# Attention scores on row tiles of 32: two heads at a time, each in a PSUM bank of its own

## The chip, the core and the metric

One core of one Trainium2 chip runs the whole program in one launch. The metric is the device time of that core in microseconds, as the median of some runs; one execution more is profiled, and all durations come from that one. A time is told from another of this kernel by about one per cent.

## What is computed

Four sequences of 256 tokens with 512 features go through two layers. In layer 0 a latent attention and a gated feed-forward net both read the same normalized input, and both are added to it. In layer 1 a selective scan (a state-space model) and a routed mixture of low-rank experts do the same. The change touches the attention of layer 0 only:

```python
C_q  = x @ Wq_d + bq_d                       # 12 latents per token
C_kv = x @ Wkv_d + bkv_d                     # 4 latents per token
q = (C_q @ W_qk + b_qk).reshape(b, s, 32, 4) # 32 heads of 4
scores = einsum('bqhd,bkd->bhqk', q, C_kv) / sqrt(4)
attn = softmax(scores, axis=-1)
V = (C_kv @ Wv_u + bv_u).reshape(b, s, 32, 16)
out = einsum('bhqk,bkhd->bqhd', attn, V).reshape(b, s, 512) @ Wo + bo
```

A head has only four numbers per token, and keys are shared by all heads.

## The kernel before

**Layout.** The 32 heads are four groups `gq` of two halves `hf` of four heads `h4`. A query tile `qs[b]` holds, on 128 partitions, four heads of 32 rows each, for every `gq` and `hf` and all 256 queries; the 32 rows of a head hold its four numbers in high and low parts, and rows for the maximum. The key tile `kms[b]` has four variants, one for each `h4`: variant `h4` is zero outside the 32 rows `32*h4` to `32*h4 + 32`. So a matmul over all 128 rows gives the scores of one head, because the rows of the other three meet zeros. Both are fp32r.

**Two sets of scores.** The scores are made twice. `scores_max` (L324) makes them with queries on the output's partitions, two matmuls of 128 x 512 into one `sc` tile of two banks, and VectorE reduces that to maxima per head (L331). `put_max` (L336) transposes the maxima and subtracts them from the queries. `attend` (L354) then makes the scores transposed, with keys on the partitions: two matmuls of 128 x 512 into one `scT` tile, and one exponential of ScalarE (L363) over both. `weigh` (L365) multiplies the exponentials by the key latents: four matmuls with 32 columns of weights each, one for every `gq`, into four quarters of the partitions of `av`. Each is fp32 and takes two passes in the trace.

**Buffers.** `sc` and `scT` share a pool of two buffers of two banks (`pssc`), so each group of scores waits until the exponential or the reduction two groups before has read its buffer.

**Order.** The order on each engine is written out by hand, as that in which the program is recorded. The feed-forward net is a generator `ff`, and `go(ff, n)` places n steps of it between the attention's instructions; a step of `gate_up` (L403) is two full matmuls of 128 x 512 (L417, the high and low part of the input), a step of `down` (L432) two as well (L442). The scores of block 0 and 2 stand in loops with one or two steps after each group. `attention` (L467) goes through eight steps `k`: `attend`, one step of `ff`, `attend`, one step, then (for blocks 0 and 2) a group of `scores_max` for the next block, `weigh` of the step before, and another group of `scores_max`, then `step - 2` steps of `ff`. `step` is 4, 2, 4 and 4 for the four blocks. `latents` (L269) makes the query and key tiles, with small matmuls of 40, 12 and 8 rows (L289, L296, L310).

After the attention come the projections, the convolution and the scan of layer 1, which the change does not touch.

Of the kernel before, what the change touches and what calls it, by code (L numbers as in the profile page):

```python
# [12 lines left out]
ALU = mybir.AluOpType  # L13
AX = mybir.AxisListType
# [3 lines left out]
P = 128  # L18
B, S, D = 4, 256, 512
# [22 lines left out]
def block_kernel(  # L42
# [25 lines left out]
    mm = nc.tensor.matmul  # L68
# [70 lines left out]
    zk = ap1.tile([P, NTB, 56], F32, name="zk")  # L139
    nc.gpsimd.memset(zk, 0.0)  # L140
    mpl2 = []
    for i in range(2):
        t = ap1.tile([P, 2, 4, 32], F32, name=f"mpl{i}")
# [123 lines left out]
    qs, kms = {}, {}  # L267
# [55 lines left out]

    def scores_max(b, j):  # L324

        gq, hf, qb = j // 4, j // 2 % 2, j % 2
        sc = pssc.tile([P, 2, 512], F32, tag="sc", name="sc")
        for hp in range(2):
            mm(sc[:, hp, :], lhsT=qs[b][:, gq, hf, qb * P : (qb + 1) * P],  # L329
               rhs=kms[b][:, 2 * hp : 2 * hp + 2, :], start=True, stop=True)  # L330
        nc.vector.tensor_reduce(  # L331
            mpl2[b % 2][:, qb, :, 16 + 2 * gq + hf].rearrange("p (a i) -> p a i", a=2),
            sc.rearrange("p a (i k) -> p a i k", i=2), AX.X, ALU.max,
        )

    def put_max(b):  # L336
# [15 lines left out]
    avs, pes = {}, {}  # L352

    def attend(b, k, t):  # L354

        c, h4 = k // 4, k % 4
        if t == 0:
            pes[b, k] = ap1.tile([P, 4, 512], F32, tag="pe", name="pe", bufs=2)
        sc = pssc.tile([P, 2, 512], F32, tag="sc", name="scT")
        for j in range(2):  # L360
            mm(sc[:, j, :], lhsT=kms[b][:, h4, c * P : (c + 1) * P], rhs=qs[b][:, 2 * t + j],  # L361
               start=True, stop=True)
        nc.scalar.activation(pes[b, k][:, 2 * t : 2 * t + 2, :], sc, AF.Exp)  # L363

    def weigh(b, k):  # L365

        c, h4 = k // 4, k % 4
        if k == 0:
            avs[b] = psav.tile([P, 2, S], F32, tag="av", name="av")
        for gq in range(4):  # L370
            mm(avs[b][32 * gq : 32 * gq + 32].rearrange("p a b -> p (a b)"),  # L371
               lhsT=zk[:, 2 * b + c, 24 - 8 * h4 : 56 - 8 * h4], rhs=pes[b, k][:, gq, :],
               start=(c == 0 and h4 == 0), stop=(c == 1 and h4 == 3))

    def normalize(b, ff):
# [91 lines left out]
    def attention(b, ff, after, first, step, side=()):  # L467

        put_max(b)
        go(ff, first)  # L470
        side = list(side)
        for k in range(8):
            attend(b, k, 0)
            go(ff, 1)
            attend(b, k, 1)
            go(ff, 1)
            if after:
                scores_max(b + 1, 2 * k)
            if k:
                weigh(b, k - 1)  # L480
            if after:
                scores_max(b + 1, 2 * k + 1)
            go(ff, step - 2)
            if side:
                f, *args = side.pop(0)
                f(*args)
        go(ff, 1)
        weigh(b, 7)
        go(ff, 1)
        normalize(b, ff)  # L490
# [34 lines left out]
    for j in range(16):  # L525
        scores_max(0, j)
        if j in (4, 8):
            fold_att(j // 8)
            go(ff, 1)
        else:  # L530
            go(ff, 2 if j % 3 else 1)
        if j % 2 == 1:
            go(second, 1)
# [53 lines left out]
    t = w_of["x", 0, 0] = w1.tile([P, 2, HC, P], F32, tag="w_in", name="w_in", bufs=3)  # L587
# [36 lines left out]
    for i in range(2):  # L624
        t = w1.tile([P, 2, KC - 1 + S], F32, name=f"pad{i}")
# [445 lines left out]
    for n in range(NG):  # L1071
        w = slice(n * NB, (n + 1) * NB)
# [32 lines left out]
    for i in range(2):  # L1105
        pdu = psmm.tile([P, 2, S], F32, tag="mm", name="pdus")
        for k in range(2):
            mm(pdu[:, k, :], lhsT=sel[:, (2 * i + k) * P : (2 * i + k + 1) * P], rhs=du[:, 0, :],
               start=True, stop=True)
# [152 lines left out]
    for u in range(total + 2):  # L1262
# [8 lines left out]
        if last >= 0 and last % NU == NU - 1:  # L1271
            c = last % PER // NU
# [9 lines left out]
        if late and u >= total - PER + 22:  # L1282
            c = late.pop(0)
# [113 lines left out]
```

## Time and profile before

| | |
|---|---|
| median of 3 runs | 893.94 us (888.75 to 894.7) |
| profiled execution, its time | 889.37 us |
| its span, first to last instruction | 887.6 us |
| mean granted TensorE clock | 0.927 |
| TensorE matmuls busy | 756.4 us (85%), 3554 |
| VectorE busy | 685.2 us (77%), 675 |
| ScalarE busy | 525.8 us (59%), 1009 |
| GpSimd busy | 489.9 us (55%), 377 |
| scores for the maxima, L329 | 128 matmuls, mean 424 ns |
| transposed scores, L361 | 128 matmuls, mean 408 ns |
| values, L371 | 256 records, mean 605 ns |
| maxima on VectorE, L331 | 64, mean 1222 ns |
| exponentials on ScalarE, L363 | 64, mean 1023 ns |

A matmul's time in such a table runs from its start to the end of its result, so neighbours overlap; what one costs in a row of matmuls is the distance of their starts. "PEld" is the load of the stationary operand, which may run beside a matmul. Rows are written as rows x columns of the stationary tile, then rows x columns that stream: `128*32 128x512` is a tile of 128 rows and 32 columns with 512 columns streamed.

### The profile page before, as it was taken

The page shows a single profiled execution, that of the slowest core. Times are in us where ns is not written, and L with a number is a line of the kernel's source. Part 1 is how long each engine was busy: PE and PEld are TensorE (multiplying, and loading weights), DVE is VectorE, ACT ScalarE, POOL GpSimd, SP SyncE. Part 2 cuts the span into 40 slices and gives each one's busy share as a digit, 9 for nine tenths or more (in the row PEclk, how much of TensorE's full clock was granted, in tenths as well). Part 3 has the DMA queues.
Part 4 walks back from the last instruction along what each step waited for, and adds up shares of the span by engine and source line. Part 5 has one row for each costly group of instructions (what it writes and reads, how often), then busy time and mean ns, then how long its engine had stood idle before and what let it go on. Part 6 is the DMA issues. An engine that isn't in the chain of part 4 may idle for free.

```text
span 887.6 us, 10460 instructions
## 1 busy us (share of the span) xinstructions
PE 756.4 (85%) x3554; PEld 434.2 (49%) x3554; DVE 685.2 (77%) x675; ACT 525.8 (59%) x1009; POOL 489.9 (55%) x377
## 2 busy tenths in 40 slices
PE   5999989999989999998687898668898777965966
PEld 3675555667556576665453444334454433422422
DVE  4695554377565333878999999999999999999995
ACT  4225445312536437678787687776786794855561
POOL 4222222001223242758967789869689759697664
PEclk9999999899999999978997999888999889989896
DMA  6232242001112231374741645341646232426200
GB/s 213 60 95 72 72 119 71 13 1 36 48 48 72 72 116 26 96 185 153 239 111 51 165 120 159 98 127 54 166 134 163 84 96 75 126 72 178 72 24 24
DMA packets 67343, 86.67 MB, mean 98 GB/s; under 512 B 12077, under 2 KB 52025, under 8 KB 66906
## 3 DMA queue, kind: packets, MB, share of 16 engines
q1 hardware_dynamic: 57930, 67.12, 27.0%
q0 software_dynamic: 9072, 18.35, 7.5%
q8 instruction: 28, 0.46, 0.2%
q10 hardware_dynamic: 288, 0.52, 0.2%
q14 instruction: 25, 0.20, 0.1%
HBM read 66.58 MB, written 10.22 MB: 87 GB/s over the span
## 4 chain that ended last, share of the span: by engine, by line
DVE 39%; PE 36%; ACT 11%; POOL 6%; issue 5%; DMA 2%; SPq 0%; DVEq 0%; ACTq 0%; POOLq 0%
DVE h L909 23%; DVE bx L894 8%; ACT decay L888 5%; PE pu L417 5%; PE pg L417 4%; POOL hc L913 4%; PE sc L329 4%; PE av L371 3%; PE po L442 3%; PE scT L361 3%; PE px L696 2%; PE po L1017 2%; ACT pe L363 1%; PE ysum L925 1%; PE pqg L319 1%
## 5 line engine op out<-in xcount | busy, mean ns | idle before, releaser
L913 POOL TENSOR_TENSOR hc<-h,cr 128x1024 f32<-128x1024 f32 (+1 forms) x131 | 301.9, 2307 | 100.6 <-DVE h L909 89.1
L909 DVE TENSOR_TENSOR_SCAN h<-decay,bx 128x1024 f32<-128x1024 f32 (+1 forms) x129 | 288.0, 2234 | 15.6 <-PE po L442 3.9
L888 ACT ACTIVATE decay<-dts,aneg 128x255 f32<-128x255 f32 x504 | 213.6, 498 | 121.0 <-DVE h L909 110.6
L925 PE MATMUL ysum<-hc,stack 128*32 128x256 f32 x1024 | 93.0, 432 | 83.8 <-POOL hc L913 83.6
L894 DVE TENSOR_TENSOR bx<-brow,dus 128x1024 f32<-128x1024 f32 x128 | 157.6, 1231 | 3.7
L429 POOL TENSOR_TENSOR hlo<-g,hhi 128x512 fp32r<-128x512 f32 x28 | 36.1, 1290 | 148.5 <-ACT hhi L428 148.5
L331 DVE TENSOR_REDUCE mpl<-sc 128x4 f32<-128x1024 f32 x64 | 77.2, 1222 | 24.1 <-PE sc L329 23.8
L925 PEld LDWEIGHTS ysum<-hc,stack 128*32 128x32 f32 x1024 | 21.8, 113 | 146.0 <-POOL hc L913 125.5
L400 POOL DMA_DIRECT2D wgu<-in_wgu x56 | 31.2, 557 | 92.7 <-PE pg L417 82.4
L363 ACT ACTIVATE pe<-scT 128x1024 f32<-128x1024 f32 x64 | 62.7, 1023 | 29.9 <-PE scT L361 29.6
L1017 PE MATMUL po<-ow,xc 128*128 128x512 f32 x128 | 73.2, 682 | 2.2 <-DVE xc L929 2.2
L857 PE MATMUL pz<-xn1T,w_in 128*128 128x256 f32 x256 | 67.0, 409 | 0.0
L696 PE MATMUL px<-xn1T,w_in 128*128 128x256 f32 x256 | 64.7, 401 | 0.7 <-DMA w_in<-in_inx 0.6
L696 PEld LDWEIGHTS px<-xn1T,w_in 128*128 128x128 f32 x256 | 51.0, 202 | 20.4 <-issue 11.1
L425 DVE SCALAR_TENSOR_TENSOR g<-g,pg 128x512 f32<-128x512 f32 x28 | 19.2, 685 | 52.0 <-ACT g L424 52.0
L857 PEld LDWEIGHTS pz<-xn1T,w_in 128*128 128x128 f32 x256 | 48.8, 200 | 18.6 <-issue 11.7
L428 ACT CAST hhi<-g 128x512 fp32r<-128x512 f32 x28 | 17.4, 620 | 61.5 <-DVE g L427 61.2
L417 PE MATMUL pg<-xhi,wgu 128*128 128x512 f32 x112 | 47.1, 421 | 5.4 <-issue 2.9
L417 PE MATMUL pu<-xhi,wgu 128*128 128x512 f32 x112 | 47.8, 427 | 1.5 <-DVE g L427 0.7
L442 PE MATMUL po<-wd,hhi 128*128 128x512 f32 x112 | 49.0, 437 | 0.0
L329 PE MATMUL sc<-km,qg 128*128 128x512 f32 x128 | 43.9, 424 | 3.3 <-ACT pe L363 2.8
L417 PE MATMUL pg<-xlo,wgu 128*128 128x512 f32 x112 | 45.7, 408 | 0.0
(225 smaller groups left out, 1256.8 us busy)
## 6 DMA issues: line engine op xcount, KB each, us to landing
dts<-dtd SPq DMA_DIRECT2D x124, 128.0 KB, 2.9
dus<-dud SPq DMA_DIRECT2D x124, 128.0 KB, 2.9
wgu<-in_wgu POOLq DMA_DIRECT2D x56, 256.0 KB, 2.7
w_in<-in_inz SPq DMA_DIRECT2D x16, 512.0 KB, 4.7
w_in<-in_inx SPq DMA_DIRECT2D x15, 512.0 KB, 4.6
dtd<-dt SPq DMA_DIRECT2D x15, 256.0 KB, 2.2
dud<-du SPq DMA_DIRECT2D x15, 256.0 KB, 2.3
wd<-in_wd POOLq DMA_DIRECT2D x7, 512.0 KB, 3.6
```

The costliest lines, as they stand in the source:

```text
L329: mm(sc[:, hp, :], lhsT=qs[b][:, gq, hf, qb * P : (qb + 1) * P], rhs=kms[b][:, 2 * hp : 2 * hp + 2, :], start=True, stop=True)
L331: nc.vector.tensor_reduce(mpl2[b % 2][:, qb, :, 16 + 2 * gq + hf].rearrange("p (a i) -> p a i", a=2), sc.rearrange("p a (i k) -> p a i k", ...
L417: mm(ps, lhsT=wgus[i][:, hc, :], rhs=xs[j][:, hc, :], start=(hc == 0 and j == 0), stop=(hc == HC - 1 and j == 1))
L442: mm(po, lhsT=hids[th][j][:, m, i * P : (i + 1) * P], rhs=wd[:, m, :], start=False, stop=(m == MC - 1 and j == 1))
L696: mm(px[:, i, :], lhsT=w[:, i, hc, :], rhs=xns[b][:, hc, :], start=(hc == 0), stop=(hc == HC - 1))
L857: mm(pz[:, i, :], lhsT=w[:, i, hc, :], rhs=xns[b][:, hc, :], start=(hc == 0), stop=(hc == HC - 1))
L888: nc.scalar.activation(da[:, k, 1:], live["dts", b, c][:, k, 1:], AF.Exp, scale=aneg[:, c, k, g : g + 1])
L894: nc.vector.tensor_tensor(bx, brow[g // 2][:, g % 2, :].unsqueeze(1).to_broadcast([P, NG, S]), live["dus", b, c], ALU.mult)
L909: nc.vector.tensor_tensor_scan(h[:, n].rearrange("p n t -> p (n t)"), da[:, n].rearrange("p n t -> p (n t)"), bx[:, n].rearrange("p n t -> ...
L913: nc.gpsimd.tensor_tensor(hc[:, n], h[:, n], crows[b][:, g, :].unsqueeze(1).to_broadcast([P, NG // parts, S]), ALU.mult,)
L925: mm(ysum[k * NB : (k + 1) * NB, :], lhsT=stack, rhs=hc[:, k, :], start=False, stop=(g == NU - 1))
L1017: mm(live["po", b, i], lhsT=xcs[b][:, c, i * P : (i + 1) * P], rhs=late_w["ow"][:, c, :], start=False, stop=(c == DC - 1))
```

## The change

Every score matmul now takes only the 32 rows of its head, from both operands, instead of all 128 with zeros in the other three quarters.

- In `scores_max` a group holds two heads `2*hp` and `2*hp + 1` in both halves `hf`, instead of four heads in one half. The two heads lie on different rows of the array and go to different banks of `sc` (index `i`), and each half takes 256 columns of a bank. A group has four matmuls of 32 x 256 instead of two of 128 x 512. The reduction reads the same 1024 numbers, and writes four maxima to other places of the same tile.
- In `attend` the two matmuls of a group would have used the same 32 rows. So head `h` is now `(gq + h4) % 4`: the two matmuls use different rows, and each has its own bank as before. `weigh` takes the slice of the key latents that fits that head, so over the steps each `gq` still meets all four heads.

The number of reductions, exponentials and groups, their order on all engines and all transfers are as before. TensorE has 128 matmuls more in its program.

```diff
@@ -323,14 +323,16 @@
 
     def scores_max(b, j):
 
-        gq, hf, qb = j // 4, j // 2 % 2, j % 2
+        gq, hp, qb = j // 4, j // 2 % 2, j % 2
         sc = pssc.tile([P, 2, 512], F32, tag="sc", name="sc")
-        for hp in range(2):
-            mm(sc[:, hp, :], lhsT=qs[b][:, gq, hf, qb * P : (qb + 1) * P],
-               rhs=kms[b][:, 2 * hp : 2 * hp + 2, :], start=True, stop=True)
+        for hf in range(2):
+            for i in range(2):
+                w = slice(64 * hp + 32 * i, 64 * hp + 32 * i + 32)
+                mm(sc[:, i, hf * S : (hf + 1) * S], lhsT=qs[b][w, gq, hf, qb * P : (qb + 1) * P],
+                   rhs=kms[b][w, 2 * hp + i, :], start=True, stop=True)
         nc.vector.tensor_reduce(
-            mpl2[b % 2][:, qb, :, 16 + 2 * gq + hf].rearrange("p (a i) -> p a i", a=2),
-            sc.rearrange("p a (i k) -> p a i k", i=2), AX.X, ALU.max,
+            mpl2[b % 2][:, qb, 2 * hp : 2 * hp + 2, 16 + 2 * gq : 18 + 2 * gq],
+            sc.rearrange("p i (f k) -> p i f k", f=2), AX.X, ALU.max,
         )
 
     def put_max(b):
@@ -353,12 +355,15 @@
 
     def attend(b, k, t):
 
+
         c, h4 = k // 4, k % 4
         if t == 0:
             pes[b, k] = ap1.tile([P, 4, 512], F32, tag="pe", name="pe", bufs=2)
         sc = pssc.tile([P, 2, 512], F32, tag="sc", name="scT")
         for j in range(2):
-            mm(sc[:, j, :], lhsT=kms[b][:, h4, c * P : (c + 1) * P], rhs=qs[b][:, 2 * t + j],
+            h = (2 * t + j + h4) % 4
+            w = slice(32 * h, 32 * h + 32)
+            mm(sc[:, j, :], lhsT=kms[b][w, h, c * P : (c + 1) * P], rhs=qs[b][w, 2 * t + j],
                start=True, stop=True)
         nc.scalar.activation(pes[b, k][:, 2 * t : 2 * t + 2, :], sc, AF.Exp)
 
@@ -368,8 +373,9 @@
         if k == 0:
             avs[b] = psav.tile([P, 2, S], F32, tag="av", name="av")
         for gq in range(4):
+            h = (gq + h4) % 4
             mm(avs[b][32 * gq : 32 * gq + 32].rearrange("p a b -> p (a b)"),
-               lhsT=zk[:, 2 * b + c, 24 - 8 * h4 : 56 - 8 * h4], rhs=pes[b, k][:, gq, :],
+               lhsT=zk[:, 2 * b + c, 24 - 8 * h : 56 - 8 * h], rhs=pes[b, k][:, gq, :],
                start=(c == 0 and h4 == 0), stop=(c == 1 and h4 == 3))
 
     def normalize(b, ff):
```

## Prediction

> **What bounds the kernel now.** The page first: the span, the share of each engine, and the slices.
>
> ```profile
> span 887.6 us, 10460 instructions
> PE   5999989999989999998687898668898777965966
> DVE  4695554377565333878999999999999999999995
> PEclk9999999899999999978997999888999889989896
> ```
>
> One slice is 22.2 us. Slices 2 to 15 (about 28 to 318 us) hold the scores and the attention, and there PE stands at 8 to 9 while DVE is mostly below 8: this part goes at TensorE's pace. From slice 20 on DVE sets the pace, and no edit lies there. So the change is priced on TensorE, stage by stage. The table of stages (us; then busy time of PE, weight load, DVE, ACT, POOL; then granted clock) confirms it:
>
> ```profile
> 28.60:58.90 30.30, 30.10 (x125) 20.47 (x123) 25.08 (x30) 8.48 (x16) 8.11 (x11) 1.00 0.30 87
> 64.10:111.70 47.60, 44.93 (x209) 27.07 (x210) 26.58 (x28) 21.72 (x27) 13.20 (x18) 1.00 0.26 74
> 217.00:262.20 45.20, 44.26 (x203) 25.29 (x202) 25.05 (x26) 21.23 (x26) 11.68 (x15) 1.00 0.22 59
> 271.00:307.00 36.00, 36.00 (x184) 21.76 (x182) 10.92 (x19) 24.30 (x30) 11.73 (x15) 1.00 0.26 69
> ```
>
> These are the scores of block 0, and the attention of blocks 0, 2 and 3. PE is busy 94 to 100%, at full clock. A busy PE includes the tail of each matmul, so prices are read from start to start, in the timeline of TensorE in block 0:
>
> ```profile
> 71.03 0.40 PE L417 MATMUL pu<-xlo,wgu 128*128 128x512 f32 x1
> 71.27 0.62 PE L329 MATMUL sc<-km,qg 128*128 128x512 f32 x2
> 71.83 1.06 PE L371 MATMUL av<-pe,zk 128*32 128x512 f32 x8
> 72.82 0.73 PE L329 MATMUL sc<-km,qg 128*128 128x512 f32 x2
> ...
> 75.94 0.40 PE L417 MATMUL pg<-xlo,wgu 128*128 128x512 f32 x1
> 77.04 0.72 PE L329 MATMUL sc<-km,qg 128*128 128x512 f32 x2 [0.70 <-ACT pe L363]
> ```
>
> Three things are read here. A full 128x512 matmul follows another after 0.23 us, so a group of two scores takes 0.462. The eight av records are four column tiles of 32 in two passes each: 0.99 us from start to start for what would be 8 x 0.43 = 3.4 one after the other, so tiles of different columns do run side by side. And where the shape of the tile changes, time is lost: sc to av takes 0.56 where two matmuls take 0.46, and the first sc behind av lasts longer. The last two lines show a wait: 1.10 us from start to start, of which 0.87 is waiting for the exponential that frees the score buffer.
>
> **The change part by part.** It takes nothing off DVE, ACT, POOL or the queues: 64 maxima over 128x1024 (1.22 us each, L331), 64 exponentials (1.02 us, L363) and the eight av records per step stay, with other columns and another slice of zk. On TensorE 128 full score matmuls L329 become 256 of 32 rows x 256 columns, and 128 of L361 become 128 of 32 rows x 512. The gain would be that two row tiles run side by side; the price is that each group of scores now has another tile shape than the full matmuls around it.
>
> *Price of a change of shape.* Before has matmuls of few rows, too, among full ones (12 rows at L296, 8 at L310):
>
> ```profile
> 19.88 1.12 PE L296 MATMUL pq<-cq,wqk 12*128 12x256 f32 x4
> 20.94 0.50 PE L417 MATMUL pg<-xhi,wgu 128*128 128x512 f32 x1
> 21.28 0.39 PE L417 MATMUL pg<-xlo,wgu 128*128 128x512 f32 x1
> 21.60 0.29 PE L310 MATMUL pz<-cst,kT 8*128 8x8 f32 x2
> 21.98 0.50 PE L417 MATMUL pu<-xhi,wgu 128*128 128x512 f32 x1
> 22.31 0.40 PE L417 MATMUL pu<-xlo,wgu 128*128 128x512 f32 x1
> ```
>
> From 21.28 to 21.60 is 0.32 instead of 0.23: 0.09 in which the array empties. The first full matmul after the change lasts 0.50 instead of 0.40, and the next follows after 0.33 to 0.34 instead of 0.23: 0.105 of weight load that nothing covers. So a change of shape costs 0.196 us, into the small tile and out of it.
>
> *How many.* In TensorE's order of the two programs, by the rows and columns of each stationary tile, the changes of shape up to the last av are 98 before and 304 after: 206 more. By stage: scores of block 0 +26, attention 0 +48, attention 1 and scores of block 2 +52, attention 2 +48, attention 3 +32. Beside av nothing is added (it was another shape already). 206 x 0.196 = 40.4 us more.
>
> *What the pairs save.* No row of before shows two row tiles side by side, so it is bounded: nothing if they run one after the other; half of the group, 0.231 us, if they overlap as the column tiles do. 128 groups x 0.231 = 29.6 us at most. Between the ends lies a load of weights that can't overlap: loads of 128 columns follow each other by 0.11 us (20.94 to 21.05 at L417), so a pair would be 0.107 longer and four small scores 4 x 0.107 = 0.43 instead of 0.231, 64 x 0.107 + 64 x 0.197 = 19.5 us lost again. I take full overlap, since av, the nearest row, has it. The Trainium skill, "TensorE: Matmul & The Clock Gate", section "Measured speedup vs the span model", gives 3.07 times for four row tiles, which no run here shows yet; by it the saving is nearer the full 29.6 than nothing.
>
> *Sum on TensorE:* 40.4 - 29.6 = +10.8 us (by stage +1.4, +2.0, +2.8, +2.0, +2.6).
>
> *What lies beside other work.* Some score groups wait anyway. From start to start such waits make 6.9 us in all: three of 0.87 in attention 0 like the one shown, 0.92 early in attention 2, 0.67 twice in attention 1, and smaller ones. The chain that ends them (tanh, product, copy, exponential on ACT and DVE) starts from a full matmul ahead of the scores and does not move; TensorE arrives later at the wait by two boundaries in and out and two shorter groups, about 0.35 us, and that is hidden. Ten or so waits by 0.3 us make 3 us. If that cover is gone the sum is +10.8; if all waits were cover, +4. I take +8.
>
> *The granted clock.* This is what could make it large. The clock is 1.00 or 0.50 in stretches of 3.41 us, and I set beside each such stretch what TensorE streamed in the one before:
>
> ```profile
> 166.72:170.13 3.41, 3.04 (x13) 1.82 (x13) 1.51 (x4) 0.85 (x2) 0.00 (x0) 1.00 0.00 0
> 170.13:173.55 3.42, 3.40 (x12) 2.54 (x12) 1.72 (x4) 0.62 (x1) 0.00 (x0) 0.50 0.00 0
> ...
> 432.95:436.36 3.41, 1.48 (x7) 0.95 (x5) 3.34 (x4) 3.34 (x9) 3.25 (x4) 1.00 0.99 299
> 436.36:439.77 3.41, 2.18 (x24) 1.31 (x24) 3.31 (x3) 1.52 (x5) 3.41 (x3) 1.00 0.94 398
> ```
>
> The first stretch has PE busy 3.04 us and yet the clock halves after it; the third has 1.48 and keeps it. In the first run four full matmuls (4 x 0.213 = 0.85 us of columns), four of 40 rows (0.43) and four of 12 rows (0.85). Weighted by rows of 128 that is 0.85 + 0.13 + 0.08 = 1.06, a share of 0.31; the third has 6.6 full ones of 0.213, a share of 0.41. Worked out so over all stretches of the trace, the clock fell after each share up to 0.36 and held from 0.38 on; from half clock it rose after 0.74 and more, and stayed after 0.73 and less. A pair of 32-row tiles counts half, so the score groups thin this share. In the steady attention loop after (8 full matmuls 1.71, av 0.85, four pairs 0.43, in 5.6 us) the mean is 0.53, and the leanest 3.41 us, around a wait cut to 0.5 us, have 1.5 / 3.41 = 0.44. The first step of attention 0 and 2 has no av: pair, two full, pair, two full, wait, scores, wait, scores: 1.18 / 3.41 = 0.35. The clock falls if a stretch lies just there (it may begin within some 0.7 of 3.41 us, about 1 in 4 for each block). At half clock the leanest no longer matters but the richest: four full ones and a part of av give 2.4 / 3.41 = 0.71, under 0.74, so it would stay until the attention ends. A step then takes about 9.8 us instead of 5.6: 7 steps x 4.2 = +30 us for that block. The Trainium skill, "TensorE: Matmul & The Clock Gate", section "HAM oscillation — how this bites in real kernels", asks only that TensorE has no idle gap over 3.4 us. There is none here, so by the page the clock costs nothing and the sum stays +8; the stretch at 166.72 speaks against it.
>
> **The rivals.**
> 1. *The clock falls in an attention and stays low:* +8 + 30, 927 on the profiled time, and 957 if in both. For it: the 0.35 above. Against: a small margin over 0.36 suffices, and where stretches begin is chance.
> 2. *Row tiles do not overlap:* the change then does not do what it says. 40.4 - 4 hidden = +36, 925, and pairs at a quarter share would lower the clock as well, 955. For it: no row shows it. Against: av.
> 3. *Faster:* a tile of 64 of 128 rows leaves half the array free, and if weights are loaded there while others stream, a boundary costs only the emptying. 206 x 0.09 = 18.5 - 29.6 = -11 us, 878. It decides from a boundary under 29.6 / 206 = 0.144 us. Against: the first matmul at 20.94 and 21.98 lasts 0.50 although 8 and 12 rows were in use.
>
> **How the numbers follow.** Forecast: overlap, boundaries paid, clock mostly held: 889.37 (profiled time, span 887.6) + 8 = 897.4. The median of the runs, 893.94, lies 4.6 above the profiled one, so as a median I expect 893.9 + 8 = 902. Its own range is 896 to 921 (serial loads at the top). Chances: forecast 0.44, clock 0.38, no overlap 0.10, faster 0.08. The range 891 to 940 leaves out the faster case and the dearest ends of the first two rivals. This kernel can be told from no change by about 1%, 8.9 us: the forecast lies at that line, so half of it counts as the same (0.22), with 0.02 from the faster case; faster 0.06; slower 0.70.
>
> **What would show it.** Right: pairs of L361's successor starting within 0.05 us of each other; the first L417 behind each at 0.50; the attention of block 3 longer by 2 to 3 us; DVE and ACT rows unchanged; the part behind 318 us only shifted. Wrong: pairs 0.2 us apart (rival 2), first full matmuls at 0.40 (rival 3), stages at granted clock well under 0.9 (rival 1).

## The result, and the profile after

The changed kernel is slower: a median of 896.37 us over 20 runs (892.9 to 907.37), beside 890.74 us for the kernel before in the same runs (886.81 to 895.09). The ratio is 1.0064, with a 95% interval of 1.0042 to 1.0086, so about 5.7 us (3.7 to 7.7): clear of no change over these runs, but less than the one per cent by which one time is told from another. Two of the 20 runs, at 905.0 and 907.4 us, had a mean granted clock of 0.919 and 0.914, the others 0.922 to 0.934. The profiled execution took 892.9 us.

The page of the changed kernel: span, TensorE's busy tenths, and the granted clock.

```profile
span 891.1 us, 10715 instructions
PE   5999989999989999998787898677998777965966
PEclk9999999999999999988997999888999889989896
```

The shape is that of before. What is new shows in the table of stages (attention 0 and attention 3):

```profile
64.10:111.70 47.60, 46.48 (x244) 22.20 (x242) 27.53 (x30) 22.22 (x27) 12.97 (x18) 1.00 0.25 73
271.00:307.00 36.00, 36.00 (x171) 16.46 (x174) 10.80 (x19) 23.86 (x28) 10.77 (x14) 1.00 0.24 64
```

In the same 36 us of attention 3 TensorE gets through 171 matmuls where it did 184, at full clock. In attention 0 it is busy 46.48 us instead of 44.93 and does not fall behind: some of its waits are gone. The timeline of TensorE in block 0 says why:

```profile
71.39 0.40 PE L423 MATMUL pu<-xlo,wgu 128*128 128x512 f32 x1
71.72 0.50 PE L366 MATMUL scT<-qg,km 32*128 32x512 f32 x2
72.14 0.50 PE L423 MATMUL pu<-xhi,wgu 128*128 128x512 f32 x1
72.48 0.40 PE L423 MATMUL pu<-xlo,wgu 128*128 128x512 f32 x1
72.81 0.50 PE L331 MATMUL sc<-km,qg 32*128 32x256 f32 x4
73.24 1.07 PE L377 MATMUL av<-pe,zk 128*32 128x512 f32 x8
...
77.67 0.39 PE L423 MATMUL pg<-xlo,wgu 128*128 128x512 f32 x1
78.23 0.50 PE L331 MATMUL sc<-km,qg 32*128 32x256 f32 x4 [0.17 <-ACT pe L368]
```

Both matmuls of a transposed group are one piece of 0.50 us, and in each of the 64 groups they start 3 to 4 ns apart: they run side by side. The group starts 0.33 us after the full matmul ahead of it instead of 0.23, the full one behind it lasts 0.50 and is followed after 0.34 instead of 0.23. From 71.39 to 72.48 is 1.09 us, where four starts 0.231 apart made 0.92. The last two lines are the wait shown for before: 0.56 from start to start, where it was 1.10.

Step by step of the attention (from one start of av to the next), before and after: in attention 0, 4.95 and 5.87 in turn became 5.17 and 5.42; in attention 2, 4.95 and 5.33 became 5.17 and 5.17; attention 1 went from 3.05 to 3.18, attention 3 from 4.00 to 4.30. By stages the span grew by 1.1 us in the scores of block 0, -0.5 in attention 0, +0.4 in attention 1, -0.5 in the scores of block 2, +0.1 in attention 2 and +2.5 in attention 3; the end is 3.5 us later. In the scores of block 2 the kernel before had a stretch of 6.8 us at half clock (from 170 us) and the changed one had none; this helps the changed kernel in the two profiles, and they do lie closer (3.5 us) than the medians.

### The profile page after: what moved, and what is told of

It reads as the page before. It is cut to its first block, busy times and chain, and to the rows that moved or that the text cites. A ratio compares the mean times of both kernels' runs of the same rounds, so it can differ in the third digit from the quotient of the medians.

```text
span 891.1 us, 10715 instructions
## 1 busy us (share of the span) xinstructions
PE 762.0 (86%) x3682; PEld 410.7 (46%) x3682; DVE 685.2 (77%) x675; ACT 527.4 (59%) x1009; POOL 489.9 (55%) x377
## 4 chain that ended last, share of the span: by engine, by line
DVE 39%; PE 34%; ACT 12%; POOL 6%; issue 6%; DMA 2%; SPq 0%; DVEq 0%; ACTq 0%; POOLq 0%
DVE h L915 24%; DVE bx L900 8%; ACT decay L894 6%; PE pu L423 5%; PE pg L423 5%; POOL hc L919 3%; PE av L377 3%; PE po L448 3%; PE sc L331 3%; PE scT L366 2%; PE px L702 2%; ACT pe L368 1%; PE po L1023 1%; DVE px L726 1%; PE pl L274 1%
## 5 line engine op out<-in xcount | busy, mean ns | idle before, releaser
L368 ACT ACTIVATE pe<-scT 128x1024 f32<-128x1024 f32 x64 | 64.3, 1024 | 30.0 <-PE scT L366 29.7
L423 PE MATMUL pg<-xhi,wgu 128*128 128x512 f32 x112 | 52.7, 471 | 5.4 <-issue 2.9
L423 PE MATMUL pu<-xhi,wgu 128*128 128x512 f32 x112 | 52.3, 467 | 1.8 <-DMA wgu<-in_wgu 0.9
L423 PE MATMUL pu<-xlo,wgu 128*128 128x512 f32 x112 | 44.4, 396 | 0.0
```

The source lines that it names most:

```text
L423: mm(ps, lhsT=wgus[i][:, hc, :], rhs=xs[j][:, hc, :], start=(hc == 0 and j == 0), stop=(hc == HC - 1 and j == 1))
```

## The experiments

The theory: each change of tile shape costs 0.196 us, pairs on two row tiles save 0.231 us, and waits for the score buffers cover a part in attention 0 and 2. The rivals: overlap is worth nothing; the cost goes by the number of matmuls; the granted clock is what costs. Ratios are to the kernel before, run beside each experiment. They are not quotients of the medians, and the two can differ by some 2 us (e8 below: 0.9978, although 885.51 stands beside 889.68).

**Each half alone.** e1 keeps the new `attend` and `weigh` and the old `scores_max`; e2 the reverse.

```diff
 # e1: scores_max
-        for hf in range(2):
-            for i in range(2):
-                w = slice(64 * hp + 32 * i, 64 * hp + 32 * i + 32)
...
+        for hp in range(2):
+            mm(sc[:, hp, :], lhsT=qs[b][:, gq, hf, qb * P : (qb + 1) * P],
+               rhs=kms[b][:, 2 * hp : 2 * hp + 2, :], start=True, stop=True)
 # e2: attend and weigh
-            h = (2 * t + j + h4) % 4
-            w = slice(32 * h, 32 * h + 32)
-            mm(sc[:, j, :], lhsT=kms[b][w, h, c * P : (c + 1) * P], rhs=qs[b][w, 2 * t + j],
+            mm(sc[:, j, :], lhsT=kms[b][:, h4, c * P : (c + 1) * P], rhs=qs[b][:, 2 * t + j],
```

> Only the transposed scores are on row tiles; the scores for the maxima are full matmuls as before. Theory (0.196 us for each change of shape, 0.231 us saved by each pair that overlaps, waits of the score buffers cover part of it in attention 0 and 2): 122 changes more x 0.196 - 64 x 0.231 = +9.1 us on TensorE; a step of attention 1 at 3.18 instead of 3.05, of attention 3 at 4.30 instead of 4.00; in attention 0 and 2 about half is covered, so +4 to +6 us against before. Rival (the two edits cost alike, by their number of matmuls): half of the measured +5.6, so +2.8.

> Only the scores for the maxima are on row tiles; the transposed ones are full as before. Theory: 84 changes more x 0.196 - 64 x 0.231 = +1.7 us on TensorE, all of it in the two loops of scores (+1.1 to +1.4 each), and -0.07 us for each step of attention 0 and 2, where they stand beside av, which has another shape anyway. Sum +1 us. Rival (alike by number of matmuls): +2.8 us or more, since this edit has all the 128 matmuls that were added.

e1: 895.27 us, ratio 1.0068 (1.0041 to 1.0094), so +6.0 us. e2: 889.77 us, ratio 1.0012 (0.9989 to 1.0034), so +1.1 us, not told from none. The transposed scores carry the loss, although only the other half has more matmuls than before: it is not their number. Steps in e1: 3.18 in attention 1, 4.30 to 4.33 in attention 3, and 5.23 in attention 0 where before had 4.95; in e2 4.84 there, 0.11 less, because a group beside av pays no additional change on that side. The long steps of attention 0, those with the wait, are 5.87 in e1 as in before, but 5.42 in e2: what made them shorter in the changed kernel is the half with the maxima.

**Overlap taken away.** e3 is the changed kernel with the same head, so the same 32 rows, in both matmuls of a transposed group.

```diff
-            h = (2 * t + j + h4) % 4
+            h = h4
...
-            h = (gq + h4) % 4
+            h = h4
```

> As the changed kernel, but both matmuls of a transposed group take the same head, so the same 32 rows: they can't run side by side. Theory (overlap is what pays for part of the changes of shape): each of 64 groups longer by 0.21 us; steps of attention 1 at 3.6 and of attention 3 at 4.7 us; 13.6 us in all, less what waits cover in attention 0 and 2: +10 to +13 us against the changed kernel, about +17 against before. Rival (a K of 32 alone matters, overlap is worth nothing): no difference to the changed kernel.

It took 931.15 us (907.48 to 937.78, 4 runs), some 35 us over the changed kernel and far more than expected. One of the four took 907.48 us, at a mean granted clock of 0.935: that is 11 us over the changed kernel, as expected. The other three had 0.898 to 0.909, and the profiled execution is one of them. TensorE's timeline in attention 1:

```profile
129.47 0.40 PE L423 MATMUL pg<-xlo,wgu 128*128 128x512 f32 x1
129.79 0.73 PE L366 MATMUL scT<-qg,km 32*128 32x512 f32 x2
130.45 0.50 PE L423 MATMUL pg<-xhi,wgu 128*128 128x512 f32 x1
```

A group now takes 0.66 us to the next start instead of 0.43, and the steps are 3.64 in attention 1 and 4.76 in attention 3, as expected: overlap is worth 0.23 us a group. The rest, in those three runs, is the clock, as the profile of one of them shows. The table of stretches, at the first step of attention 2 and behind it:

```profile
227.87:231.28 3.41, 2.60 (x15) 1.54 (x14) 2.15 (x3) 1.15 (x2) 0.88 (x2) 1.00 0.58 156
...
231.30:289.30 58.00, 58.00 (x167) 25.36 (x166) 19.08 (x19) 15.92 (x18) 7.02 (x9) 0.50 0.11 28
```

The first stretch has a row-weighted share of about 0.35, worked out as in the prediction; then 58 us go at half clock, with a step of attention 2 at 9.9 us, as rival 1 had priced it. The shares in these 58 us are 0.45 to about 0.75, and the clock comes back after one of about 0.77.

**Double the rows.** e4 has the pairs on tiles of 64 rows, half of them zeros, with the heads of a pair in different halves of the array.

```diff
-            h = (2 * t + j + h4) % 4
-            w = slice(32 * h, 32 * h + 32)
+            h = (t + 2 * j + h4) % 4
+            w = slice(64 * (h // 2), 64 * (h // 2) + 64)
...
-                w = slice(64 * hp + 32 * i, 64 * hp + 32 * i + 32)
+                w = slice(64 * i, 64 * i + 64)
```

> As the changed kernel, but with tiles of 64 rows (32 of them zeros), heads paired so that the two are in different halves of the array. Same changes of shape, same overlap, twice the share of rows. Theory: within 1 us of the changed kernel (+5.6 against before), with no run above 900, since the share of rows that holds the clock is far from its limit. Rival (the lower share of rows costs clock in every run): faster than the changed kernel by 3 us or more.

896.05 us, ratio 1.0069 (1.0039 to 1.0098), steps as in the changed kernel to 0.03 us. So the lower share of rows is not what the changed kernel loses by in its median. One of ten runs took 900.9, just over what the theory had named, so that part is not settled.

**What covered the change.** In e5 (from the kernel before) and e6 (from the changed one) half of the exponentials are left out, which shortens each on ScalarE; TensorE's work stays the same.

```diff
-        nc.scalar.activation(pes[b, k][:, 2 * t : 2 * t + 2, :], sc, AF.Exp)
+        nc.scalar.activation(pes[b, k][:, 2 * t : 2 * t + 2, 0:S], sc[:, :, 0:S], AF.Exp)
...
-               ... rhs=pes[b, k][:, gq, :],
+               ... rhs=pes[b, k][:, gq, 0:S].unsqueeze(1).to_broadcast([P, 2, S]),
```

> The kernel before with each exponential over the first 256 of every 512 columns only, and the values made from these columns twice; half of the exponentials are left out. This takes about 0.4 us off each of 64 exponentials, so the waits for the score buffer that end on ScalarE should go: a pair of steps in attention 0 at 9.9 to 10.0 instead of 10.8 us. Theory: 5 us faster than before. Rival (the reductions on VectorE end these waits): no change.

> The changed kernel with the same half of the exponentials left out. Theory (waits for the exponential were the cover that hid the change in attention 0 and 2): without them the difference to the half kernel of before grows to nearly the sum on TensorE, +9 to +11 us, and every step of attention 0 and 2 is 0.2 us longer than there. Rival (the cover lies in the reductions): the difference stays at 4 to 6 us.

e5: 884.51 us, ratio 0.9952 (0.9921 to 0.9984). e6: 893.18 us, ratio 1.0057 (1.0030 to 1.0084). Between them lie 8.7 us by the medians, and 9.3 by the two ratios, instead of 5.7. In attention 2 the steps are 4.92 in e5 and 5.17 in e6: with the waits gone, the change shows in full, 0.25 us a step. In attention 0 e5 has 4.92 and 5.46, not the 9.9 to 10.0 a pair that was expected: half of the wait of 0.87 stays (0.44), and the pair is no shorter than e6's. So the exponentials are the cover in attention 2, and about half of it in attention 0. What the rest is can be read in the traces. These are the links that end the long wait of attention 0, in the kernel before and in the changed one:

```profile
73.59 1.23 DVE L331 TENSOR_REDUCE mpl<-sc 128x4 f32<-128x1024 f32 x1 [0.43 <-PE sc L329]
75.44 0.62 ACT L428 CAST hhi<-g 128x512 fp32r<-128x512 f32 x1 [3.41 <-DVE g L427]
75.97 1.93 ACT L363 ACTIVATE pe<-scT 128x1024 f32<-128x1024 f32 x2
...
74.78 1.22 DVE L333 TENSOR_REDUCE mpl<-sc 128x4 f32<-128x1024 f32 x1 [0.20 <-PE sc L331]
76.63 0.62 ACT L434 CAST hhi<-g 128x512 fp32r<-128x512 f32 x1 [3.35 <-DVE g L433]
77.16 1.93 ACT L368 ACTIVATE pe<-scT 128x1024 f32<-128x1024 f32 x2
```

The chain begins with the reduction of the score group behind av. The product of the feed-forward net stands behind it on VectorE (0.68 us), its copy and then the exponential follow on ScalarE, and only the first exponential frees the buffer. From the start of the reduction to the score matmul that waited it takes 3.45 us in both kernels (73.59 to 77.04, 74.78 to 78.23). In e5 it takes 3.02, shorter by what the exponential lost; the wait that is left lies in the reduction, the product and the copy.

**Another order.** e7 is the control: before, with full matmuls, but in attention 1 and 3 the values of two steps earlier, both transposed groups and the feed-forward steps stand in blocks. e8 has the same order, and row tiles for the transposed scores of these two blocks alone.

```diff
+                if k > 1:
+                    weigh(b, k - 2)
+                attend(b, k, 0)
+                attend(b, k, 1)
+                go(ff, step)
...
 # e8 besides
+            h = (2 * t + j + h4) % 4 if b % 2 else h4
+            w = slice(32 * h, 32 * h + 32) if b % 2 else slice(0, P)
```

> The kernel before (full matmuls), but in attention 1 and 3 the values of two steps earlier come first, then both transposed groups at once, then the feed-forward steps together. The same matmuls and as many changes of shape as before. Theory: the same as before within 1 us; steps at 3.05 and 4.0 us. It is the control for the next one. Rival: with both groups side by side the exponential comes late, and steps of attention 1 get longer by 0.3 us or more.

> The order of the control, and in attention 1 and 3 alone the transposed scores on row tiles as in the changed kernel; all else full as before. Both groups and av now stand together, so a step has one change of shape more than before, for two overlapped pairs. Theory: 0.196 - 0.462 = -0.27 us for each of 16 steps, -4.3 us: steps of 2.8 and 3.75 us, faster than before by 3 to 5 us. Rival (row tiles cost time wherever they are used): slower than the control.

e7: 887.8 us, ratio 0.9981 (0.9960 to 1.0003), steps as before. e8: 885.51 us, ratio 0.9978 (0.9956 to 1.0000): some 2 us faster by the ratio where 3 to 5 were expected, and by the times not told from the control. Its steps are 2.57 and 3.48 us, though, 0.5 shorter than the control's and more than two pairs explain. TensorE in attention 1 of e8:

```profile
128.17 0.53 PE L364 MATMUL scT<-qg,km 32*128 32x512 f32 x4
128.62 0.51 PE L421 MATMUL pu<-xhi,wgu 128*128 128x512 f32 x1
...
129.76 1.07 PE L375 MATMUL av<-pe,zk 128*32 128x512 f32 x8
130.76 0.51 PE L364 MATMUL scT<-qg,km 32*128 32x512 f32 x4
```

All four transposed matmuls are one piece of 0.5 us: their heads lie on four different row tiles, so four run side by side in the time of one. That is 0.69 - 0.196 = 0.49 us a step. In the profiled runs the projections behind the attention begin 5.4 us earlier than before, and the end comes 4.0 us earlier.

**The clock by itself.** e9 is the kernel before with 80 matmuls of 32 x 512 ahead of attention 0, in pairs on two row tiles, and 40 ahead of attention 2 on one.

```diff
+    def rowtest(n, b):
+        ps = [psmm.tile([P, 512], F32, tag="mm", name="rt") for _ in range(2)]
+        for r in range(80 // (3 - n)):
+            i = r % n
+            w = slice(32 * i, 32 * i + 32)
+            mm(ps[i], lhsT=kms[b][w, i, 0:P], rhs=qs[b][w, 0], start=True, stop=True)
```

> The kernel before with 80 more matmuls of 32 rows x 512 columns ahead of attention 0, in pairs on two row tiles, and 40 more ahead of attention 2, all on one row tile; their results are not used. TensorE has nothing else in these stretches of 9 us and is busy all the time. Theory (the clock goes by streamed time weighted by rows, falling under 0.37): pairs have a share of 0.5 and keep 1.00, matmuls start in twos every 0.22 us; singles have 0.25, and after 3.4 to 6.8 us the clock halves and they start every 0.43 us. Rival (the clock goes by busy time, or by idle gaps): 1.00 in both.

One stretch of the pairs, then the first full stretch of the singles and the one behind it:

```profile
65.48:68.89 3.41, 3.41 (x31) 3.04 (x27) 0.00 (x0) 0.00 (x0) 0.00 (x0) 1.00 0.00 0
...
219.90:223.36 3.46, 3.46 (x16) 2.73 (x16) 0.61 (x1) 0.00 (x0) 0.00 (x0) 1.00 0.00 0
223.36:226.78 3.42, 3.42 (x10) 2.62 (x9) 0.00 (x0) 0.00 (x0) 0.00 (x0) 0.50 0.00 0
```

TensorE is busy without a gap in all three. The pairs keep the clock, and two matmuls take 0.23 us together. The singles start 0.23 us apart, and 3.6 us after the first the clock halves; from there they start 0.43 us apart, for the 10 us that are left. Busy time can't tell these apart, rows do.

**Four at once, everywhere.** e10 puts the transposed scores of all blocks on row tiles, both groups of a step together; the scores for the maxima are full, as before.

```diff
+                attend(b, k, 0)
+                attend(b, k, 1)
+                go(ff, 2)
+                scores_max(b + 1, 2 * k)
+                go(ff, 1)
+                scores_max(b + 1, 2 * k + 1)
+                go(ff, step - 3)
+                weigh(b, k)
```

> The transposed scores of all four blocks on row tiles, both groups of a step next to each other, so that four row tiles may run side by side (the steps of the reordered kernel were 0.2 us shorter than two pairs explain); the scores for the maxima stay full. In attention 0 and 2 a step is: both transposed groups, four full matmuls, a group of maxima, two full, a group of maxima, two full, values. One change of shape more than before for four overlapped matmuls: 0.196 - 0.69 = -0.49 us on TensorE for each step. Theory: attention 1 and 3 as in the reordered kernel (2.57 and 3.5 us a step); in attention 0 and 2 steps of 4.6 to 5.0 us instead of 5.1 and 5.4 on the mean, since the two score buffers still bind; 6 to 9 us faster than before. Rival (the buffers bind wholly: the second group waits for the reduction of the last maxima): steps of 5.2 us or more there, no better than the reordered kernel.

883.59 us (12 runs), ratio 0.9939 (0.9910 to 0.9967): about 5.4 us faster than before (4.0 by the medians, 887.57 for before), a little less than expected. The steps that the theory asked for in attention 0 and 2 were not reached: 5.12 to 5.18 in attention 0, where before has 4.95 and 5.87 in turn, and 4.73 and 5.76 in attention 2, where before has 4.95 and 5.33. On the mean the steps are 5.14 and 5.25 us, where before has 5.41 and 5.14, and the rival, that the buffers bind, had said 5.2 or more: by its steps it mostly holds there. TensorE's timeline in attention 0:

```profile
75.68 0.50 PE L364 MATMUL scT<-qg,km 32*128 32x512 f32 x2
76.40 0.50 PE L364 MATMUL scT<-qg,km 32*128 32x512 f32 x2 [0.22 <-DVE mpl L331]
```

The second group waits until VectorE has reduced the last maxima, and the two groups no longer overlap. The stages are shorter all the same. From its first transposed group to its last av, attention 0 takes 41.4 us where before has 43.8, attention 2 takes 42.3 instead of 43.0, attention 1 26.0 instead of 26.7, and attention 3 30.3 instead of 33.2. In e8 the same stretches are 43.8, 42.9, 24.5 and 30.2. So the gain does not come from attention 1 and 3 alone: attention 0 is shorter by 2.3 us, too. Attention 1 is longer here than in e8 because a stretch of 3.4 us in it goes at half clock (from 140.9 us), behind a stretch with a wait of 1.3 us in it and a row-weighted share of 0.31.

**A mix, and the four again.** e11 is e8 with one thing more: in attention 0 and 2 the scores for the maxima of the next block are on row tiles, where two of their groups stand beside av. e12 is e10's kernel, run a second time beside it.

```diff
     def scores_max(b, j):
+        if b % 2:
+            return scores_max_rows(b, j)
```

> The reordered kernel with row tiles in attention 1 and 3, and besides, in attention 0 and 2, the scores for the maxima (for the next block) on row tiles, where they stand on both sides of av, which has another shape anyway; the loops of scores stay full. From the kernel with the maxima alone: steps of attention 0 at 4.84 and 5.42, of attention 2 at 4.84 and 5.36, so 2 us less in attention 0 and nothing in attention 2. Theory: 0.7% to 0.9% faster than before, 2 us faster than the reordered kernel was. Rival (what is gained on TensorE in attention 0 is lost in the waits behind it): no better than the reordered kernel, 0.2% faster than before.

> The kernel with four row tiles at once in all blocks again, on the same chip as the mixed one. Its steps in attention 0 and 2 (5.15 and 5.25 us on the mean) are no better than those of the reordered kernel together (5.41 and 5.14). Theory: 0.4% to 0.6% faster than before, 1 to 3 us slower than the mixed one. Rival (that it was faster came from the reordering of attention 0 and 2): 0.6% or more, and not slower than the mixed one.

e11: 884.93 us (12 runs), ratio 0.9926 (0.9895 to 0.9958). e12: 882.84 us (12 runs), ratio 0.9923 (0.9892 to 0.9954), beside 889.77 us for the kernel before. e11's steps are as expected, 5.42 and 4.84 in attention 0 and 2. TensorE in attention 0 of e11 shows how the maxima lean on av:

```profile
92.34 0.50 PE L331 MATMUL sc<-km,qg 32*128 32x256 f32 x4
92.77 1.06 PE L392 MATMUL av<-pe,zk 128*32 128x512 f32 x8
93.77 0.50 PE L331 MATMUL sc<-km,qg 32*128 32x256 f32 x4
```

Three small pieces follow one another: sc, av, sc. The maxima add no change of shape here, since av has one ahead of it and one behind it in any case. Both versions beat the kernel before and the changed one beyond their intervals, and cannot be told from each other: that the mix is the faster by 1 to 3 us is not borne out. For e12 it is the rival that came in (0.6% or more, and not slower than the mix): its attention 0 takes 41.5 us, 2.3 less than before, as in e10, beside 42.0 in e11. What they share is the four transposed matmuls side by side in attention 1 and 3, and a shorter attention 0. Why e8, which has these too, stands at 0.9978 and e11 at 0.9926, with steps in attention 0 and 2 that explain some 2 us, stays open; the two intervals touch, and they were not run side by side. How much of the shorter attention 0 of e10 and e12 comes from the order, and how much from the row tiles, was not tried: no run has their order in attention 0 and 2 with full matmuls.

## Why the prediction was right, point by point

- *A change of shape costs 0.196 us.* Right: 0.33 instead of 0.23 ahead of the small tile, 0.42 instead of 0.23 from the overlapped pair to the full matmul behind it, and 0.34 instead of 0.23 behind that one, 0.40 for the two changes. Attention 1 grew by 0.13 a step (3 x 0.196 - 0.462 = 0.126), attention 3 by 0.30 (4 x 0.196 - 0.462 = 0.32), the shorter steps of attention 0 by 0.22 (6 x 0.196 - 0.924 = 0.25).
- *Pairs overlap, as the column tiles do.* Right, with starts 3 to 4 ns apart; e3 shows what it is worth, 0.23 us a group. Rival 2 falls, and loads of weights in a row of 0.107 each with it.
- *Cover of 3 us.* This is the term that was mis-sized. +10.8 on TensorE made 5.7 in the end (3.7 to 7.7), so about 5 us were covered. Of the 5.6 us by which 902 lies over 896.4, some 2.3 come from here, and 3.2 from the median of before, which was 890.7 in the longer series instead of 893.9. By stages the span grew by -0.5 us in attention 0 and +0.1 in attention 2, where the sum on TensorE had +2.0 each. I let each wait of 0.87 shrink by 0.35; it shrank by 0.63, to 0.24. The step that failed is where the chain that ends the wait begins: not at a full matmul ahead of the scores, but at the reduction of the score group behind av. That group is itself one of the changed ones. It ends 0.22 us earlier after the start of av (1.54 instead of 1.76 to the reduction), the chain of 3.45 is the same, and the group ahead of the next av takes 0.43 instead of 0.65. So the long steps of attention 0 went from 5.87 to 5.42, shorter and not merely covered, and more than paid for the short ones (4.95 to 5.17); e1 and e2 show that this is the maxima's half. In attention 2 the exponentials are the cover (e5 and e6).
- *The number.* That 896.4 lies in the range says little, since 891 to 940 holds the old median of 893.9, too. The +5.7 beside the forecast of +8 says more, and the stages say most. That no attention of the profiled run fell to half clock was in part luck, as the prediction had said. By the line of 8.9 us that the prediction drew, the change counts as the same, to which it gave 0.22; its likeliest answer, slower at 0.70, is borne out in direction only.
- *The clock mostly holds.* Right in the profiled run: the leanest stretch of its attention has a share of about 0.43, a little over what held before, where 0.35 was thought possible. (By their starts the third stretch of the prediction's table holds six full matmuls and not 6.6: a share of 0.38 instead of 0.41, which still lies above the 0.36.) The mechanism and its prices were right, too: e9 shows it by itself, and e3 its cost of 58 us at half clock. Whether it is what made two runs take 905 and 907 us is argued by their clock, not shown.
- *Rival 3, load hidden by the free rows.* It falls: the full matmul behind a group lasts 0.50 everywhere.
- *Nothing else moves.* Right: 64 maxima at 1.22 us, 64 exponentials at 1.02, and the part behind 318 us only shifted (3.3 us at its first projection, 3.5 at the end).

## What to carry to other kernels

Row tiles pay by how many run side by side between two changes of tile shape: a pair saves one full matmul (0.23 us here) and two changes cost 0.39, so pairs set singly among full matmuls lose, and four next to each other, or a group beside work that has another shape anyway, gain (the versions that use these, e10 with e12 and e11, reach ratios of 0.992 to 0.994, in e10 and e12 with another order besides). Before such a change count the changes of shape in the order of the matmuls, not the matmuls. An engine that sets the pace of a stage may still have waits in every second step, and these swallow what is added, and would swallow what is saved. Ask which instruction starts the chain that ends such a wait: if the change makes that one end earlier, the step gets shorter with it.

## What was not expected of the hardware

- Four row tiles in two PSUM buffers overlap fully: four 32x512 matmuls in one piece of 0.5 us, in the time of one (e8).
- The granted clock goes by the rows in use, not by busy time: TensorE without a gap on 32 rows fell to half clock after 3.6 us and stayed there; on two times 32 rows it kept the full one (e9). Over the stretches of 3.41 us in the traces of before, after and e3, worked out as in the prediction, the clock fell after row-weighted shares of up to about 0.36 and came back after about 0.75 and more, so a stretch in between stays as it is, for 58 us in e3. The rule of the Trainium skill that the prediction cited ("TensorE: Matmul & The Clock Gate", section "HAM oscillation — how this bites in real kernels"), that the clock needs only TensorE without idle gaps over 3.4 us, does not agree with these runs; the measurement decides.
